# Third stage of a convolution block: the out-projection's second tile in banks of its own, ahead of the variance

## The chip, the cores and the metric

One core of one Trainium2 chip runs the whole program. The metric is the device time of one launch in microseconds; of the kernel before there are three timed runs, and their median is 3697.74 us (3695.79 to 3697.99). The profile shows one more execution. Engines are called TensorE (PE, with its weight loads as PEld), VectorE (DVE), ScalarE (ACT), GpSimd (POOL) and SyncE (SP, which only issues DMAs here).

## The reference

The input is 16 images of 192 channels, 64 x 64 pixels, float32. Cut to what matters:

```
h  = layernorm_channels(x)                       # first stage
p, g = split(conv1x1(h, in_proj))
p  = dwconv3(p)                                  # second stage
mixed = (scan in four directions(p) + dwconv3(p)) * sigmoid(g)
mixed = gelu(batchnorm(mixed))                   # third stage from here
x  = x + conv1x1(mixed, out_proj)                # 192 -> 192
h2 = layernorm_channels(x)
x  = x + conv1x1(gelu(conv1x1(h2, fc1)), fc2)    # 192 -> 768 -> 192
# second layer: per group of images a squeeze of the pooled x gives the
# taps of a masked 3x3 depthwise filter (4 taps are not masked)
pooled = mean(x);  t = relu(bn(pooled @ w1.T));  w = t @ w2.T + b2
out = depthwise(x, w) + bias
```

The first stage and the batch normalisation's statistics need all images before the third stage can begin; the pooled mean needs a whole image before its filter can.

## The kernel before

Three stages run one after the other. The first (to about 630 us) and the second (to about 1302 us) are not touched. The third works on pairs of images: the two images lie on partitions 0 to 63 and 64 to 127 (`HALF`), and the 192 channels are three tiles of 64 (t = 0, 1, 2). A chunk is 8 rows of 64 pixels, 512 columns (`CH`, its half `HCH`); there are 8 chunks a pair and 8 pairs, so 64 iterations of the main loop, from 1333 to about 3663 us, and then a tail with the last pair's filter.

Iteration n is a software pipeline. It holds, in the order in which it is written, which is the order on every engine's queue (the schedule is manual):

- `final(n - 1)`: VectorE adds the second MLP product of the previous chunk to the image (L992).
- `first(n, m)`, m = 0 to 5: TensorE multiplies the normalised h by 128 hidden channels (12 matmuls of 64 x 64 weights, each of which the trace shows as two, four running at a time in the quadrants), and ScalarE makes the GELU of it into `gl` (L972, L974). Each takes a pair of PSUM banks.
- between these: `mean` of chunk n + 1 (L928), `center` (L940), `squares` (L948 on ScalarE, L949 and L920 on VectorE).
- `unmix(n + 3)` and `load_mixed(n + 4)`: VectorE transposes and SP's DMAs for the mixed input of later chunks.
- `piece()`: one piece of the dynamic filter of an earlier pair, if there is one: a ScalarE step (L1029), three VectorE steps (L65), and output DMAs issued by GpSimd (L1033). Of the 64 iterations, 42 have a piece at this place, 42 one later (between the parts of `second`).
- the out-projection of chunk n + 2: `out_quarters` takes the 64 channels of the third input tile (64 x 64 weights, L890), `out_columns` the other 128 (128 x 64 weights, L897); each for three output tiles t, each output tile in two halves of 256 columns in two banks.
- `mean(n + 1, ..., "sq")`, the variance of chunk n + 1, in two banks called `ps_v` (L928).
- `load(n + 3)`: SP loads x.
- `squeeze`, when a pair has ended (eight times), L1006, L1008.
- `normalize(n + 1)`: ScalarE takes the square root of the variance (a table load and two steps, L958) and goes back to GELU's table (L960); VectorE takes the reciprocal (L961) and scales h (L962).
- `residual` of chunk n + 2: VectorE adds x and the bias to the out-projection, two steps a tile (L903), and makes the channel sums on the way (L909, L920).
- `bn_gelu(n + 3)`: ScalarE makes the GELU of the mixed input (L870, L871).
- `second(n, k)`, k = 0 to 2: the second MLP product, 128 x 64 weights, two hidden tiles m by three output tiles t in each (L843, the matmuls of `both`).

PSUM has eight banks here: tag `f1` two pairs, tag `f2` three single banks, tag `a` one. A tile taken under a tag gets the tag's next buffer in turn and waits for that buffer's last readers. In the kernel before, `f1` is taken eight times an iteration (six times by `first`, then twice for the out-projection: tiles 0 and 2 share one pair, tile 1 has the other, which the sixth `first` held last). `f2` is taken seven times: two for the mean, two for the variance, three for `second`. `a` serves the squeeze and the taps.

## Time and profile before

| | |
|---|---|
| median of three runs | 3697.74 us |
| profiled execution, its own time | 3699.46 us |
| its span, first to last instruction | 3697.7 us |
| granted TensorE clock | 0.995 |
| first and second stage | 0 to 1302 us |
| main loop of the third stage | 1333.2 to 3663.7 us |
| TensorE busy in the main loop | 2325.4 of 2330.5 us |
| VectorE busy in the main loop | 1529.1 us |
| ScalarE busy in the main loop | 951.7 us |
| one undisturbed iteration | 36.19 us |

In the lines of the profile, a group of instructions is given by source line, engine, operation and the program's names as output <- inputs; "x16" is how many were merged, and a bracket names how long the engine had been idle before and what released it. Starts count from the span's first instruction. Matmuls are pipelined and their ends are modelled, so that starts say more than lengths. "PEld" is the queue of weight loads, which runs ahead of the matmuls.

### The profile page before, as it was taken

Reading aid. Unit: us, or ns where it says so; the run is one execution under the profiler, and the core shown is the slowest. Engines: PE = TensorE matmul, PEld = TensorE weight load, DVE = VectorE, ACT = ScalarE, POOL = GpSimd, SP = SyncE. Lnnn points to the kernel's source line nnn. Section 1 sums busy time; section 2 is a strip of 40 time slices with the busy share of each in tenths; the row PEclk is TensorE's granted clock in tenths of the full one; section 3 lists DMA queues with packets and bytes.
Section 4 is the critical chain, followed back from the end, with each engine's and each line's share of the span. In section 5 each row is a group of like instructions: output and inputs, shape, how many; then the busy total and the mean of one; then the engine's idle time right before and its main releaser. Section 6 shows DMA issues by size and latency. Waiting matters only on the chain.

```text
span 3697.7 us, 71384 instructions
## 1 busy us (share of the span) xinstructions
PE 3670.5 (99%) x30354; PEld 1715.5 (46%) x30354; DVE 2705.5 (73%) x4138; ACT 1791.1 (48%) x2004; POOL 420.6 (11%) x685
## 2 busy tenths in 40 slices
PE   9999999999999999999999999999999999999998
PEld 6666666555566643333333334333333334333333
DVE  6878776999999965556766757766766676775764
ACT  3433333988888843434343434444443434343432
POOL 2434332111111020000000000000000000000000
PEclk9999999999999999999999999999999999999999
DMA  6898998999999941122212212221322231222212
GB/s 163 242 255 246 261 278 247 295 294 290 281 282 283 248 97 40 27 61 68 69 51 79 72 47 70 77 61 52 85 65 54 68 82 52 68 75 55 72 38 75
DMA packets 290335, 491.82 MB, mean 133 GB/s; under 512 B 26584, under 2 KB 184784, under 8 KB 290016
## 3 DMA queue, kind: packets, MB, share of 16 engines
q1 hardware_dynamic: 232540, 296.22, 30.1%
q0 software_dynamic: 56544, 189.99, 18.7%
q8 instruction: 240, 3.93, 0.5%
q10 hardware_dynamic: 932, 1.03, 0.1%
q14 instruction: 79, 0.65, 0.1%
HBM read 284.95 MB, written 197.92 MB: 131 GB/s over the span
## 4 chain that ended last, share of the span: by engine, by line
PE 98%; DMA 1%; DVE 1%; issue 0%; ACT 0%; SPq 0%; ACTq 0%; POOL 0%
PE ps_f L972 27%; PE ps_f L843 27%; PE ps_pj L514 14%; PE ps_l L673 11%; PE ps_d L629 7%; PE ps_o L897 5%; PE ps_o L890 3%; PE ps_xt L485 2%; PE ps_m L928 1%; PE ps_v L928 1%; DMA xa<-in_x_dram 1%; PE ps_k L843 0%; DVE o L65 0%; PE pb_h L141 0%; DVE ol L65 0%
## 5 line engine op out<-in xcount | busy, mean ns | idle before, releaser
L974 ACT ACTIVATE gl<-ps_f,bf 128x1024 f32<-128x1024 f32 x384 | 427.9, 1114 | 1308.4 <-PE ps_f L972 1302.8
L972 PE MATMUL ps_f<-h,wf 64*64 64x512 f32 x9216 | 1014.9, 590 | 2.0 <-DVE h L962 2.0
L843 PE MATMUL ps_f<-gl,place 128*64 128x512 f32 x4608 | 1003.6, 593 | 2.8 <-ACT rs L958 2.8
L972 PEld LDWEIGHTS ps_f<-h,wf 64*64 64x64 f32 x9216 | 346.3, 133 | 627.9 <-issue 566.0
L843 PEld LDWEIGHTS ps_f<-gl,place 128*64 128x64 f32 x4608 | 335.3, 137 | 627.1 <-issue 614.9
L514 PE MATMUL ps_pj<-wi,xa 64*128 64x384 f32 x3072 | 517.0, 489 | 1.4 <-DVE mid L519 1.0
L65 DVE SCALAR_TENSOR_TENSOR o<-ximg,taps,o 128x1024 f32<-128x1024 f32 (+1 forms) x267 | 338.2, 1267 | 111.0 <-ACT o L1029 101.1
L514 PEld LDWEIGHTS ps_pj<-wi,xa 64*128 64x128 f32 x3072 | 292.8, 188 | 197.3 <-issue 12.7
L1033 POOL DMA_DIRECT2D out_dram<-o x168 | 90.1, 541 | 2028.4 <-DVE o L65 2025.5
L940 DVE TENSOR_TENSOR h<-ximg,ps_m 128x768 f32<-128x768 f32 x128 | 116.4, 951 | 264.6 <-PE ps_m L928 263.4
L961 DVE RECIPROCAL rs<-rs 128x512 f32<-128x512 f32 x64 | 214.3, 3349 | 53.5 <-ACT rs L958 53.5
L992 DVE SCALAR_TENSOR_TENSOR ximg<-ps_f,pt,ximg 128x512 f32<-128x512 f32 x192 | 138.6, 750 | 133.9 <-PE ps_f L843 128.1
L664 DVE TENSOR_TENSOR_SCAN v<-tab,q 128x1024 f32<-128x1024 f32 x96 | 218.3, 2274 | 7.4 <-DMA pg_d<-mid 7.4
L666 DVE TENSOR_TENSOR_SCAN v<-tab,q 128x1024 f32<-128x1024 f32 x96 | 217.6, 2266 | 0.0
L652 ACT ACTIVATE tab<-mask,dec_b 128x1024 f32<-128x1024 f32 x192 | 209.9, 1147 | 0.0
L520 ACT ACTIVATE mid<-ps_pj,rsa 128x384 f32<-128x384 f32 x128 | 119.9, 938 | 185.5 <-PE ps_pj L514 179.2
L520 ACT ACTIVATE stg<-ps_pj,rsa 128x384 f32<-128x384 f32 x128 | 119.6, 936 | 182.3 <-PE ps_pj L514 175.5
L949 DVE TENSOR_TENSOR low<-low 128x512 f32<-128x512 f32 x63 | 43.6, 693 | 209.2 <-ACT low L948 209.2
L492 DVE BATCH_NORM_STATS2 st<-ps_xt 128x6 f32<-128x192 f32 x512 | 174.1, 340 | 16.1 <-PE ps_xt L485 15.3
L897 PE MATMUL ps_o<-low,wo 128*64 128x256 f32 x1536 | 181.8, 384 | 0.0
L243 DVE STREAM_TRANSPOSE low<-low 128x512 f32<-128x512 f32 x174 | 169.0, 1026 | 2.1 <-issue 0.3
L903 DVE SCALAR_TENSOR_TENSOR ximg<-ps_o,pt,low 128x256 f32<-128x256 f32 x384 | 161.7, 476 | 2.4 <-PE ps_o L890 2.3
(213 smaller groups left out, 4181.8 us busy)
## 6 DMA issues: line engine op xcount, KB each, us to landing
low<-in_x_dram SPq DMA_DIRECT2D x128, 384.0 KB
out_dram<-o POOLq DMA_DIRECT2D x168, 256.0 KB, 3.8
mid<-pg_d SPq DMA_DIRECT2D x8, 4096.0 KB
low<-mixed_d SPq DMA_DIRECT2D x116, 256.0 KB
low<-pg_d SPq DMA_DIRECT2D x7, 4096.0 KB
pg_o<-pg_d SPq DMA_DIRECT2D x7, 4096.0 KB
xa<-in_x_dram POOLq DMA_DIRECT2D x192, 128.0 KB, 5.4
xa<-in_x_dram SPq DMA_DIRECT2D x192, 128.0 KB
```

What stands on the lines that cost most here:

```text
L65: nc.vector.scalar_tensor_tensor(o, in0, scalar, in1, ALU.mult, ALU.add, **kw)
L514: nc.tensor.matmul(ps[i], pixels(n, t, g)[q], wi[q, t].rearrange("p g k c -> p (g k c)"), start=(t == 0), stop=(t == 2))
L520: nc.scalar.activation(stag[blk][1][:, :, j], ps[1], AF.Copy, scale=rs[:, g, 1:2])
L629: nc.tensor.matmul(dst(ps[o, ih]), mats[g % 2]["dm"][q, di + 1, :, ch], src(s["pg"][q, :, 0, ch]), start=(di == 0), stop=stop)
L664: nc.vector.tensor_tensor_scan(vf, tab, q, 0.0, ALU.mult, ALU.add)
L666: nc.vector.tensor_tensor_scan(vf[:, ::-1], tab[:, ::-1], q[:, ::-1], 0.0, ALU.mult, ALU.add)
L673: nc.tensor.matmul(dst(bst[k]["ps"][o, i]), lm_of(g)[q, m, :, c], src(q, ih), start=start, stop=stop)
L843: nc.tensor.matmul(ps[q], w(i), rhs(i), start=start, stop=stop)
L897: nc.tensor.matmul(ps[wh][q].rearrange("p (r w) -> p r w", w=32), wo[:, 64 * t:64 * t + 64], cols(rows(s["mx"][:, i]))[:, :, wh], start=fi ...
L961: nc.vector.reciprocal(rs, rs)
L972: nc.tensor.matmul(pf[o, i], wf1[q, t, m0:m0 + 64], s["h"][q, t], start=(t == 0), stop=(t == 2))
L974: nc.scalar.activation(gl, pf, AF.Gelu, bias=bf1[:, m:m + 1])
```

## The change

The sixth `first` moves behind `unmix`, `load_mixed` and the piece. The out-projection takes only one pair of `f1`, for tiles 0 and 2; tile 1 gets one bank of `f2` and the bank `a`. The quarters of tile 1 go ahead of the variance, those of tiles 0 and 2 behind it. The columns are taken in the order 1, 0, 2, and the residual of tile 1 goes ahead of `normalize`. The squeeze takes a pair of `f1` instead of bank `a`. `second` renames its three banks, so that the one that tile 1 of the out-projection held comes last, and its first third works tile by tile instead of hidden tile by hidden tile. `f1` is now taken seven times an iteration (eight with a squeeze), `f2` eight times. The channel sum is made after whichever of tiles 0 and 1 is added last. In iteration 0 the GELU of chunk 2's mixed input goes from behind the fifth `first` to behind the fourth.

```diff
@@ residual
-        if t == 1:
+        s["added"] = s.get("added", ()) + (t,)
+        if t < 2 and len(s["added"]) == 2:
             s["sum"] = hp2.tile([128, 3, HCH], F32, tag="sm", name="sm", bufs=1)
@@ second
+        gl = {m: s.pop(("gl", m)) for m in (2 * k, 2 * k + 1)}
         if k == 0:
-            s["po"] = [ps2.tile([128, CH], F32, tag="f2", name="ps_f2", bufs=3) for _ in range(3)]
-        for m in (2 * k, 2 * k + 1):
-            gl = s.pop(("gl", m))
-            for t in range(3):
-                both(s["po"][t], ..., m == 0, m == NFC - 1)
+            po = [ps2.tile([128, CH], F32, tag="f2", name="ps_f2", bufs=3) for _ in range(3)]
+            s["po"] = po[1:] + po[:1]
+            order = [(m, t) for t in range(3) for m in gl]
+        else:
+            order = [(m, t) for m in gl for t in range(3)]
+        for m, t in order:
+            both(s["po"][t], ..., m == 0, m == NFC - 1)
@@ squeeze
-        pt = ps2.tile([128, CH], F32, tag="a", name="ps_t")
+        pt = ps2.tile([128, 2, CH], F32, tag="f1", name="ps_t", bufs=2)[:, 0]
@@ main loop
-        for m in range(3, NFC):
+        for m in range(3, NFC - 1):
             at(first, n, m)
-            if n == 0 and m == 4:
+            if n == 0 and m == 3:
                 bn_gelu(2)
         at(unmix, n + 3)
         at(load_mixed, n + 4)
         piece()
+        at(first, n, NFC - 1)
         po = []
         if n + 2 < n_ch:
-            pair = [ps2.tile([128, 2, CH], F32, tag="f1", name="ps_o", bufs=2) for _ in range(2)]
-            po = [[pair[j][:, wh, c0:c0 + HCH] for wh in range(2)] for j, c0 in ((0, 0), (1, 0), (0, HCH))]
-            for t in (0, 2):
-                out_quarters(n + 2, t, po[t], True, t < 2)
+            own = [ps2.tile([128, CH], F32, tag="f2", name="ps_o1", bufs=3)[:, 0:HCH],
+                   ps2.tile([128, CH], F32, tag="a", name="ps_o1")[:, 0:HCH]]
+            pair = ps2.tile([128, 2, CH], F32, tag="f1", name="ps_o", bufs=2)
+            po = [[pair[:, wh, 0:HCH] for wh in range(2)], own, [pair[:, wh, HCH:CH] for wh in range(2)]]
+            out_quarters(n + 2, 1, po[1], True)
         if n + 1 < n_ch:
             st[n + 1]["pw"] = two_banks("ps_v")
             mean(n + 1, st[n + 1]["pw"], "sq")
         at(load, n + 3)
-        if n + 2 < n_ch:
-            out_quarters(n + 2, 1, po[1], True)
+        if po:
+            for t in (0, 2):
+                out_quarters(n + 2, t, po[t], True, t < 2)
         if ended is not None:
             squeeze(ended)
-        for t in range(len(po)):
-            out_columns(n + 2, t, po[t], False, t > 0)
+        if po:
+            for t in (1, 0, 2):
+                out_columns(n + 2, t, po[t], False, t > 0)
+            residual(n + 2, 1, po[1])
         at(normalize, n + 1)
-        for t in range(len(po)):
-            residual(n + 2, t, po[t])
+        if po:
+            for t in (0, 2):
+                residual(n + 2, t, po[t])
```

More of the change, by code (lines that the diff above doesn't have):

```diff
@@ L978, in second @@
         s = st[n]
+        gl = {m: s.pop(("gl", m)) for m in (2 * k, 2 * k + 1)}
         if k == 0:
-            s["po"] = [ps2.tile([128, CH], F32, tag="f2", name="ps_f2", bufs=3) for _ in range(3)]
-        for m in (2 * k, 2 * k + 1):
-            gl = s.pop(("gl", m))
-            for t in range(3):
-                both(s["po"][t], lambda i: wf2[:, m, 64 * t:64 * t + 64], lambda i: gl[:, i], m == 0, m == NFC - 1)
+            po = [ps2.tile([128, CH], F32, tag="f2", name="ps_f2", bufs=3) for _ in range(3)]
[4 more added lines that the diff above has]
+        for m, t in order:
+            both(s["po"][t], lambda i: wf2[:, m, 64 * t:64 * t + 64], lambda i: gl[m][:, i], m == 0, m == NFC - 1)
     def final(n):
```

## The prediction

> **What bounds the kernel now.** I read the page first: busy shares, then the chain that ended last.

> ```profile
> PE 3670.5 (99%) x30354; PEld 1715.5 (46%) x30354; DVE 2705.5 (73%) x4138; ACT 1791.1 (48%) x2004; POOL 420.6 (11%) x685
> ...
> PE 98%; DMA 1%; DVE 1%; issue 0%; ACT 0%; SPq 0%; ACTq 0%; POOL 0%
> ```

> TensorE sets the end, and the diff neither adds nor removes a matmul. So the change is worth the holes that it closes or opens in TensorE's stream, and the hole can be invisible in the busy share, because modelled matmul ends (376 ns each, while a group of four starts every 0.22 us) cover it. The weight loads show it better. Of the waits of PEld in the whole span, these belong to the third stage's loop:

> ```profile
> PEld ps_f L972 <- PE ps_f L843: 50.3, 62, 0.8
> PEld ps_o L890 <- ACT gl L974: 28.0, 61, 0.7
> PEld ps_f L843 <- ACT rs L958: 3.9, 2, 3.7
> ```

> The first stands at the turn from `second` to the next `first`, which the diff leaves alone. The second is the wait that the diff aims at: 61 times, 0.46 us each, of which a part would be idle anyway (loads run ahead of matmuls). How much is real, I read from the timeline of one iteration (n = 29), weight loads, then matmuls, then ScalarE; columns are start, length, engine, line.

> ```profile
> 2405.79 0.37 PEld L928 LDWEIGHTS ps_v<-low,mean 64*64 64x64 f32 x8
> 2406.61 0.21 PEld L890 LDWEIGHTS ps_o<-low,wo 64*64 64x64 f32 x8 [0.46 <-ACT gl L974]
> 2407.21 1.06 PEld L897 LDWEIGHTS ps_o<-low,wo 128*64 128x64 f32 x12 [0.38 <-issue]
> ```

> ```profile
> 2405.14 1.04 PE L890 MATMUL ps_o<-low,wo 64*64 64x256 f32 x16
> 2406.01 0.61 PE L928 MATMUL ps_v<-low,mean 64*64 64x256 f32 x8
> 2406.62 0.66 PE L890 MATMUL ps_o<-low,wo 64*64 64x256 f32 x8
> 2407.21 1.30 PE L897 MATMUL ps_o<-low,wo 128*64 128x256 f32 x10
> ```

> ```profile
> 2405.45 1.11 ACT L974 ACTIVATE gl<-ps_f,bf 128x1024 f32<-128x1024 f32 x1 [1.46 <-PE ps_f L972]
> 2406.46 1.23 ACT L1029 ACTIVATE o<-ximg,pt,taps 128x1024 f32<-128x1024 f32 x1
> 2407.71 1.28 ACT L958 ACT_TABLE_LOAD   x1
> 2409.01 0.84 ACT L958 ACTIVATE rs<-ps_v,eps 128x256 f32<-128x256 f32 x2
> ```

> Sixteen quarter matmuls (tiles 0 and 2) take 2406.01 - 2405.14 = 0.87, or 0.216 a group of four. The eight of the variance should take 0.43, but the next start is 0.61 later: the quarters of tile 1 wait for the sixth GELU, whose bank they take over and which ends at 2406.56. From variance to columns it is 1.20. The first iteration has the same instructions without that wait:

> ```profile
> 1350.72 0.61 PE L928 MATMUL ps_v<-low,mean 64*64 64x256 f32 x8
> 1351.16 0.61 PE L890 MATMUL ps_o<-low,wo 64*64 64x256 f32 x8
> 1351.70 2.81 PE L897 MATMUL ps_o<-low,wo 128*64 128x256 f32 x24
> ```

> There it is 0.98. The hole is thus 0.22 by these rounded starts (0.230 from the unrounded ones): 0.18 of waiting, 0.05 because the load behind the wait is no longer hidden. It is the same in every iteration from 1 to 61, with or without a piece of the dynamic filter; the period is 36.19.

> [...] the columns' first load (128 rows after 64) comes about 0.1 after the last quarter group's slot, in both samples; [...]. [...] The trace shows them in the order of the code, so the piece's ScalarE step, emitted ahead of the sixth GELU, runs ahead of it. [...] The load is 1.28 here; [...] (the square root follows 0.02 later), so I count 1.30.

> **The change, part by part** (t = 0 is the first quarter matmul, 2405.14 above).

> *Tile 1's quarters ahead, in banks of their own.* Removed: the wait. The order becomes quarters 1 (two groups), variance (two), quarters 0 and 2 (four), columns: 8 x 0.216 = 1.73, [...]. The pair of banks for 0 and 2 waits for the fifth GELU (2402.87 + 1.11 = 2403.98), done before t = 0. Tile 1's banks: one of the three of tag f2, last read by `final` at the iteration's start, some 13 us before; and the single bank of tag a, last read by tile 1's own residual or by the taps' addition a whole iteration before. No new wait. Gain 0.23 in each of 61 iterations: 14.0.

> *The variance, 0.43 earlier.* Its sums were ready 3.26 before it started in these iterations; now 2.83. Hidden.

> *Piece, unmix and mixed load ahead of the sixth `first`.* On TensorE nothing moves. On SP the loads keep their order, and SP never waits for `first`. POOL's output issues wait for the piece's VectorE steps and come up to 2 us earlier. On ScalarE the piece's step (1.23) goes to 2403.98-2405.21, a hole before the GELU at 2405.45: cover 0.24. Beyond it the GELU slips. VectorE's three piece steps start after the transposes, at 2405.68 instead of 2407.73.

> *Square root and `second`.* ScalarE: GELU till 1.42, table load till 2.72, square roots till 3.19 and 3.57. `second` now starts with a bank that the first square root reads, at 1.73 + 0.11 + 2.64 (columns, 2409.85 - 2407.21) = 4.48. Slack 1.29; nothing.

> *Residual of tile 1 ahead of the reciprocal.* VectorE: piece steps till 2409.60 (4.46), residual 0.95 till 5.4; its columns, first in order now, are done by about 3.1. The third tile of `second` takes over its bank at 4.48 + two tiles of 1.72 = 7.92: slack 2.5. The reciprocal starts at 5.4 rather than at 6.43 (2411.57), so the normalised h, needed 20 us after t = 0, is not late. The same additions are made; the residual moves past no queue other than VectorE's and issues no DMA.

> *Rotation of f2.* Eight takings an iteration instead of seven: the next means take the banks of tiles 2 and 0 of `second` instead of 0 and 1, so they wait for `final`'s last step, which ended at least 3.08 before the mean in every iteration. Hidden.

> *Squeeze in f1, eight times in all.* It takes the sixth GELU's bank at t = 1.73, free at 1.42 plus some 0.05. Hidden; seven of these iterations are among the 61 and gain alike.

> *Other order within `second`'s first third.* The same matmuls; consecutive ones already accumulate in one bank. I take 0; bounded by -1 to +3 over the run, an estimate from its 0.43 cadence, which shows no hole to lose or fill.

> *Iteration 0.* Its quarters start 0.65 late, at 1349.81, for the GELU of the mixed input (two steps, about 2.0), which the diff puts one GELU earlier, into a hole. Gain about 0.7. *Iteration 62* (no out-projection): `second` waits about 3.0 for the square root; the piece's step moves ahead of the GELU (1.2 gained), but `second` no longer has a free tile to begin with (0.86 lost). Gain 0.3.

> **Sum:** 14.0 + 0.7 + 0.3 = 15.0. On the profiled execution's span, 3697.7 - 15.0 = 3682.7 (its time was 3699.46, 1.8 around the span). The unprofiled median is 3697.74, so 3682.7 for it too: 0.41% faster. 0.2% (7.4 us) is about what a measurement of this kernel can tell from no change.

> **Rivals.** *(a) The square root takes the wait over.* If the piece's step still came between GELU and table load, the first square root would end at 3.47 + 0.87 + 0.47 = 4.81 against 4.48: a stall of 0.33, some 0.38 with the exposed load, in the 41 of the 61 iterations with a piece there: 15.6 lost, 3698. For it: it is the longest chain near the turn. Against: the 1.29 of slack, as ScalarE runs in order and its hole fits the step.

> *(b) Slower: the residual is late for its bank.* In-order VectorE reaches residual 1 after the piece's 3.92. Slack 2.5; beyond it each microsecond costs 41 us. It decides when the residual ends 3.1 later than reckoned: 0.6 x 41 = 24.6 eats the 15.0 and makes 3707. For it: two engines' orders meet there, and the bank is lent for the shortest time. Against: VectorE waited 2.04 for the piece's ScalarE step, and loses that wait.

> *(c) The change does not do what it says.* If the quarters met another unfinished reader, the gain would stay out: 3697. Against: the rotation counted above. *(d) Half:* the wait moves to the pair or the squeeze, or a refilled load pipeline costs the same again: 3690.

> **Chances.** Forecast 0.83 (3680 to 3687: 11 without the exposed load, 1 each for the rest, measuring noise of 1 to 2; up to 17 gained), (d) 0.06, (a) and (c) 0.05, (b) 0.06. Faster by over 0.2% is the forecast and half of (d), 0.86; within it the other half with (a) and (c), 0.08; slower 0.06. For 8 in 10, and because (d) starts where the forecast ends: 3679 to 3690.

> **What would show it.** Right: quarters in the order 1, variance, 0, 2 with no wait on a GELU; variance to columns 1.41 (0.43 + 0.87 + 0.11) and first quarter to columns 1.84 instead of 2.07; period 35.96; ScalarE's piece step ahead of the sixth GELU. Wrong: weight loads of `second` waiting for L958 or for a residual, of the means for L992, or ScalarE's sixth GELU starting late behind a piece that waits for its output buffer.

## The result and the profile after

The changed kernel takes 3676.51 us (median of five runs, 3674.51 to 3678.68) against 3696.90 us for the kernel before beside it (five runs): a ratio of 0.9945 with an interval of 0.9934 to 0.9956. It is faster by 0.55%, 20.4 us; the forecast was 15.0 us, with 3679 to 3690 for 8 in 10. A second set gave 3674.65 (five runs), with 3695.05 for the kernel before (13 runs): 20.4 again.

The page of the changed kernel, busy shares and the chain that ended last by engine:

```profile
PE 3649.8 (99%) x30354; PEld 1724.1 (47%) x30354; DVE 2713.3 (74%) x4138; ACT 1792.0 (49%) x2004; POOL 419.3 (11%) x685
...
PE 90%; DVE 1%; DMA 0%; issue 0%; ACT 0%; ACTq 0%; SPq 0%; POOL 0%; DVEq 0%
```

The number of matmuls is the same, and TensorE is still the bound. (The chain's 90%, where it was 98%, is no sign of a new bound: it is followed through less of the first stage, whose `ps_pj` has 7.5% of it instead of 13.5%.) Waits of the weight loads over the span, those of the third stage's loop:

```profile
PEld ps_f L973 <- DVE ximg L997: 51.1, 63, 0.8
PEld ps_t L1011 <- ACT gl L975: 2.7, 7, 0.4
PEld ps_f L843 <- ACT rs L959: 1.7, 1, 1.7
```

The row of 61 waits of `ps_o` for the GELU is gone. The first row is the turn from `second` to the next `first`; it was 50.3 in 62 waits and is now put down to `final` instead of to the matmuls, with the same 0.8 each. The 2.7 at the squeeze was there before too, but was put down to "issue", that is, to no wait that the profile shows. Iteration 29 again, matmuls and then ScalarE:

```profile
2393.03 0.61 PE L890 MATMUL ps_o<-low,wo 64*64 64x256 f32 x8
2393.46 0.61 PE L929 MATMUL ps_v<-low,mean 64*64 64x256 f32 x8
2393.89 1.04 PE L890 MATMUL ps_o<-low,wo 64*64 64x256 f32 x16
2394.86 2.81 PE L897 MATMUL ps_o<-low,wo 128*64 128x256 f32 x24
2397.50 4.89 PE L843 MATMUL ps_f<-gl,place 128*64 128x512 f32 x22
```

```profile
2391.77 1.23 ACT L1034 ACTIVATE o<-ximg,pt,taps 128x1024 f32<-128x1024 f32 x1
2393.33 1.12 ACT L975 ACTIVATE gl<-ps_f,bf 128x1024 f32<-128x1024 f32 x1 [0.33 <-PE ps_f L973]
2394.47 1.28 ACT L959 ACT_TABLE_LOAD   x1
2395.76 0.84 ACT L959 ACTIVATE rs<-ps_v,eps 128x256 f32<-128x256 f32 x2
```

First quarter to columns takes 1.83 instead of 2.07, the piece's step sits ahead of the sixth GELU, and the first square root is done at about 2396.2, some 1.3 before `second` starts.

Since the loop is so regular, the two traces can be subtracted iteration by iteration, from the start of one `first` to that of the next:

| part of the loop | before | after | difference |
|---|---|---|---|
| iteration 0 | 36.68 | 35.96 | -0.72 |
| an iteration from 1 to 61 (seven with a squeeze: 38.10, 37.87) | 36.19 | 35.96 | -0.23, in all -14.03 |
| iteration 13, on top of that | 0.28 | 0 | -0.28 |
| iteration 62 | 36.76 | 33.08 | -3.68 |
| iteration 63 | 35.85 | 35.93 | +0.08 |
| whole loop, to the first matmul of the tail's filter | 2330.51 | 2311.87 | -18.64 |

So 18.6 of the 20.4 lie in the loop, and iteration 62, which I had given 0.3, holds 3.68. The 0.28 of iteration 13 is a later sixth GELU in both traces of the kernel before. It comes with the piece's place behind that GELU: it is gone where the piece alone is moved, and back where the piece is put back (both below). What delays the GELU stays open. The stretch before the loop and the tail differ too, but they differ as much between two traces of one kernel: the loop began at 1333.2 and at 1326.7 in two traces of the kernel before, and the tail took 32.3 and 34.3 in two of the changed one. The 1.8 that are left are within the interval of the ratio; no run tells what they are.

### The profile page after: what moved, and what is told of

Read it like the earlier page. It is cut to its first block, busy times and chain, and to the rows that moved or that the text cites. A ratio compares the mean times of both kernels' runs of the same rounds, so it can differ in the third digit from the quotient of the medians.

```text
span 3672.7 us, 71322 instructions
## 1 busy us (share of the span) xinstructions
PE 3649.8 (99%) x30354; PEld 1724.1 (47%) x30354; DVE 2713.3 (74%) x4138; ACT 1792.0 (49%) x2004; POOL 419.3 (11%) x685
## 3 DMA queue, kind: packets, MB, share of 16 engines
q8 instruction: 239, 3.92, 0.5%
## 4 chain that ended last, share of the span: by engine, by line
PE 90%; DVE 1%; DMA 0%; issue 0%; ACT 0%; ACTq 0%; SPq 0%; POOL 0%; DVEq 0%
PE ps_f L973 27%; PE ps_f L843 27%; PE ps_l L673 11%; PE ps_pj L514 7%; PE ps_d L629 7%; PE ps_o L897 5%; PE ps_o L890 2%; PE ps_xt L485 1%; PE ps_m L929 1%; PE ps_v L929 1%; PE ps_k L843 0%; DMA xa<-in_x_dram 0%; DVE o L65 0%; PE pb_h L141 0%; DVE ol L65 0%
## 5 line engine op out<-in xcount | busy, mean ns | idle before, releaser
L843 PE MATMUL ps_f<-gl,place 128*64 128x512 f32 x4608 | 1001.9, 592 | 0.8 <-ACT rs L959 0.8
L843 PEld LDWEIGHTS ps_f<-gl,place 128*64 128x64 f32 x4608 | 334.9, 137 | 623.8 <-issue 613.9
L897 PE MATMUL ps_o<-low,wo 128*64 128x256 f32 x1536 | 182.0, 385 | 0.2 <-ACT low L870 0.2
```

The source lines that it names most:

```text
L843: nc.tensor.matmul(ps[q], w(i), rhs(i), start=start, stop=stop)
L897: nc.tensor.matmul(ps[wh][q].rearrange("p (r w) -> p r w", w=32), wo[:, 64 * t:64 * t + 64], cols(rows(s["mx"][:, i]))[:, :, wh], start=fi ...
```

## The experiments

A "stall" is here the distance from one start of TensorE's matmuls to the next, less the 0.43 that a group takes anyway; the expectations round the 2.93 of iteration 62 to 3.0.

*Theory after the result:* the steady part is as forecast; iteration 62 of the kernel before loses 2.9 to a wait for the square root, and then 1.7 more because TensorE's clock fell behind that wait. *Rivals:* the piece's new place, or the residual's, or the place of the quarters gains throughout the loop; the slow groups of iteration 62 are a refill of the pipeline; part of the gain is the luck of one profile.

**Part alone: the piece's place.** In the kernel before:

```diff
-        for m in range(3, NFC):
+        for m in range(3, NFC - 1):
             at(first, n, m)
-            if n == 0 and m == 4:
+            if n == 0 and m == 3:
...
         piece()
+        at(first, n, NFC - 1)
```

> The kernel before, with only the sixth `first` put behind the piece (and iteration 0's GELU of the mixed input one place earlier); banks and order of the out-projection as before. Theory (the hole is the wait for the sixth GELU's bank, and the clock fell after iteration 62's stall): the period stays 36.19, because the sixth GELU still ends 1.42 after the first quarter and tile 1 still waits; iteration 0 is 0.5 shorter; in iteration 62 the first square root ends 1.15 earlier, the stall shrinks from 3.0 to about 1.8, and if the clock then stays up another 1.7 goes: 2 to 4 us faster in all, about 3693.5 to 3695. Rival (the piece's place is what gains, by the earlier square root): a period near 35.96 and 3683 or less.

Measured: 3692.08 against 3696.02, ratio 0.9989 (0.9981 to 0.9998). The period stayed 36.19; iteration 0 took 36.13 (-0.55), iteration 62 took 33.94 (-2.82, that is 1.13 for the earlier square root and 1.69 because the clock, of which more below, stayed up). The weight loads of the quarters wait as before:

```profile
PEld ps_o L890 <- ACT gl L974: 28.3, 62, 0.5
```

So the place alone gains nothing in the steady loop, 3.4 at its two ends, and the 0.28 of iteration 13, which took 36.19 here. The time is 3.9 lower than that of the kernel before, inside the 2 to 4 that I had expected.

**Undone part: the piece behind the sixth `first`.** In the changed kernel, the sixth `first` goes back ahead of the piece (iteration 0's GELU of the mixed input stays where the change put it):

```diff
-        for m in range(3, NFC - 1):
+        for m in range(3, NFC):
...
         piece()
-        at(first, n, NFC - 1)
```

> The changed kernel, with the sixth `first` back ahead of the piece. Theory, from the trace's durations: in the 41 of 61 iterations with a piece there the first square root ends 4.81 after the first quarter, and `second` asks for its bank at 4.48, so TensorE stalls 0.33 to 0.38: period 36.3 there, 35.96 in the 20 without a piece; with some 1 to 3 more in iteration 62, 15 to 19 us slower than the changed kernel, 3691 to 3696. Rival (the order on ScalarE does not matter, slack covers it): 3676 to 3678 and a period of 35.96 throughout.

Measured: 3678.06, 1.55 above the changed kernel's first median, and a period of 35.96 except in iteration 13 (36.20). My expectation was wrong, and the rival right. The trace shows why (ScalarE, then a weight load of `second`):

```profile
2359.93 1.28 ACT L959 ACT_TABLE_LOAD   x1
2361.23 0.84 ACT L959 ACTIVATE rs<-ps_v,eps 128x256 f32<-128x256 f32 x2
```

```profile
2361.75 0.24 PEld L843 LDWEIGHTS ps_f<-gl,place 128*64 128x64 f32 x4 [0.20 <-ACT rs L959]
```

The first quarter of this iteration starts at 2357.36, so the first square root (0.47 of the 0.84) ends about 4.34 after it, not at 4.81: the 3.47 of my sum, counted from the variance, was already its end, and I had added its 0.47 once more. The weight load waits for it, but `second` still starts 2.64 after the columns, as ever. But hardly anything is left: in iteration 13, where the GELU came 0.28 late, `second` came 0.24 late. So the order on ScalarE is worth about 1.2 us of slack in the steady loop and no time, except in iteration 13; it is worth 1.13 in iteration 62, which took 34.20 here.

**Undone part: the quarters' place.** Changed kernel, with tile 1's quarters behind the variance and the other two, in banks of their own still:

```diff
-            out_quarters(n + 2, 1, po[1], True)
+            for t in (0, 2):
+                out_quarters(n + 2, t, po[t], True, t < 2)
...
         if po:
-            for t in (0, 2):
-                out_quarters(n + 2, t, po[t], True, t < 2)
+            out_quarters(n + 2, 1, po[1], True)
```

> The changed kernel, with tile 1's quarters at their old place, behind the variance and behind tiles 0 and 2, but still in the banks of their own. Theory (the bank makes the wait, not the place): no wait on a GELU, period 35.96, 3676.5 within 0.1%. Rival (the place ahead of the variance gains, because the variance or the square root comes sooner or later): a period that differs by 0.05 or more, above 3680.

Measured: 3677.41, period 35.96, no wait of `ps_o` for `gl`. The banks make the gain; that the quarters stand ahead of the variance adds nothing that can be seen. (Iteration 0 took 37.66, because a stretch of half clock, of which more below, fell into it.)

**Undone part: the residual's place.** Changed kernel, all three residuals behind the reciprocal and the scaling:

```diff
-            residual(n + 2, 1, po[1])
         at(normalize, n + 1)
         if po:
-            for t in (0, 2):
+            for t in (1, 0, 2):
                 residual(n + 2, t, po[t])
```

> The changed kernel, with the residual of tile 1 behind the reciprocal and the scaling, next to the other two. Theory of the lent bank: in iterations with a piece VectorE ends that residual at about 10.45 after the first quarter, and `second` asks for the bank at 7.92: a stall of 2.5 to 2.6 in 41 iterations (107), and of about 1.75 in the 20 without a piece (35): about 142 us slower, 3819. If stalls of that length also lower TensorE's clock, as I read iteration 62 of the kernel before, up to 1.7 more in each of the longer ones: 3819 to 3890. Rival (the residual's place is free, since VectorE has time): 3676 to 3680.

Measured: 3785.42, ratio 1.0245 (1.0229 to 1.0260), slower than the changed kernel by 109 (the loops of the two traces differ by 108.6) where I had expected about 142. Iterations with a piece took 37.97 (+2.01; only iteration 61 took less, 37.54), those without 37.30 (+1.34), those with a squeeze 38.94 (+1.07). VectorE and the weight loads of one iteration:

```profile
2370.39 3.35 DVE L962 RECIPROCAL rs<-rs 128x512 f32<-128x512 f32 x1
2373.77 1.76 DVE L963 TENSOR_TENSOR h<-h,rs 128x1536 f32<-128x1536 f32 x1
2375.45 1.65 DVE L903 SCALAR_TENSOR_TENSOR ximg<-ps_o,pt,low 128x256 f32<-128x256 f32 x4
```

```profile
2375.98 0.20 PEld L843 LDWEIGHTS ps_f<-gl,place 128*64 128x64 f32 x4 [2.68 <-DVE ximg L903]
```

The load goes on 0.53 after the residual's start, so it waits for the first of its two steps alone (0.48): the second step reads bank a, which `second` doesn't take. That is the 0.4 to 0.5 by which I had made the stalls too long; those with a squeeze, which I had not priced apart, are shorter still. The bank is lent at the price of this order: with the residual behind the reciprocal, the change would have been a loss of about 2.4%. None of the 40 stalls of 2.0 here lowered the clock; the granted clock is 1.0 from 1310.8 to 3747.9 in this trace.

**The clock: fill the gap.** In the kernel before, idle matmuls in iteration 62 alone, whose result nobody reads:

```diff
+        if n == n_ch - 2:
+            idle(3)
         at(normalize, n + 1)
```

> The kernel before, with three idle matmuls (128 x 128 weights, 512 columns, nobody reads their result) in iteration 62 alone, between the variance and `second`, inside the stall of 3.0. Theory (the stall lets TensorE's clock fall, and the half clock costs 1.7): the stall still ends with the first square root, but the groups behind it start every 0.43 at once, without the four starts of 0.86: iteration 62 is 1.5 to 1.8 shorter, 3695.3. It shows in the trace's granted clock around that place; in the median of the runs only if no other half-clock window comes and goes. Rival (the slow groups are a refill of the pipeline after the wait, whatever the clock): iteration 62 as long as before or up to 1 longer.

Measured: iteration 62 took 35.07 instead of 36.76: 1.70 shorter by the unrounded starts, with the weight load still waiting for the same square root. The median was 3693.21 against 3696.24, ratio 0.9993 (0.9985 to 1.0001), which alone would not tell. The weight loads of `second` in the second trace of the kernel before, and then in this one:

```profile
3604.86 0.20 PEld L843 LDWEIGHTS ps_f<-gl,place 128*64 128x64 f32 x4 [3.65 <-ACT rs L958]
3605.35 0.14 PEld L843 LDWEIGHTS ps_f<-gl,place 128*64 128x64 f32 x2 [0.28 <-ACT rs L958]
3605.95 0.24 PEld L843 LDWEIGHTS ps_f<-gl,place 128*64 128x64 f32 x2 [0.46 <-issue]
3606.81 0.24 PEld L843 LDWEIGHTS ps_f<-gl,place 128*64 128x64 f32 x2 [0.61 <-issue]
```

```profile
3608.46 0.20 PEld L843 LDWEIGHTS ps_f<-gl,place 128*64 128x64 f32 x4 [0.88 <-ACT rs L958]
3608.95 0.14 PEld L843 LDWEIGHTS ps_f<-gl,place 128*64 128x64 f32 x2 [0.29 <-ACT rs L958]
3609.38 0.14 PEld L843 LDWEIGHTS ps_f<-gl,place 128*64 128x64 f32 x2 [0.29 <-issue]
3609.80 0.14 PEld L843 LDWEIGHTS ps_f<-gl,place 128*64 128x64 f32 x2 [0.29 <-issue]
```

In the first, two loads come at the usual distance, and then the distance doubles to 0.86 and a load takes 0.24 instead of 0.14. The granted clock in the second trace of the kernel before, ahead of this stretch, in it and behind it (columns: window, length, busy time of PE, PEld, DVE, ACT and POOL, each with its number of instructions, then the clock, the DMA share and GB/s):

```profile
3602.18:3605.59 3.41, 0.72 (x4) 0.34 (x6) 2.49 (x2) 3.36 (x5) 0.00 (x0) 1.00 0.00 0
3605.60:3609.00 3.40, 3.40 (x10) 0.98 (x8) 3.36 (x3) 1.08 (x2) 1.07 (x2) 0.50 0.18 40
3609.00:3612.40 3.40, 3.40 (x18) 1.15 (x16) 3.01 (x2) 0.00 (x0) 0.00 (x0) 1.00 0.44 114
```

Half the clock for 3.41 costs 1.7. Against a refill of the pipeline: the first two loads behind the wait keep the usual distance, and behind the stall of 2.1 of the next experiment the pace is the usual one from the start, so that rival falls. Nor did the filled gap lie otherwise against the clock's steps of 3.41 (see the last section): it would have lain from 3605.69 to 3608.46, wholly inside one step (3605.13 to 3608.54, counted from the changes of the clock in that trace), as it lies, but for 0.09, in the kernel before.

**Part alone: tile by tile.** In the kernel before, only the order in `second`'s first third:

```diff
-        for m in (2 * k, 2 * k + 1):
-            gl = s.pop(("gl", m))
-            for t in range(3):
-                both(s["po"][t], ..., m == 0, m == NFC - 1)
+        gl = {m: s.pop(("gl", m)) for m in (2 * k, 2 * k + 1)}
+        order = [(m, t) for t in range(3) for m in gl] if k == 0 else [(m, t) for m in gl for t in range(3)]
+        for m, t in order:
+            both(s["po"][t], ..., m == 0, m == NFC - 1)
```

> The kernel before, with only the order in the first third of `second` changed: tile by tile. Theory: no hole anywhere but in iteration 62, so a period of 36.19; in iteration 62 two blocks instead of one run before the wait for the first square root, so that it is 0.86 shorter, and 2.5 if the stall of 2.1 that is left no longer lowers the clock: 3696.0 or 3694.4. Rival (consecutive accumulation into one bank costs): a longer period, from 36.2 up.

Measured: 3693.21 against 3696.24, ratio 0.9991 (0.9983 to 1.0000). The period stayed 36.19 and iteration 62 took 34.21 (-2.55): 0.86 for the second block ahead of the wait, and 1.69 because the clock stayed up over the 2.07 that were left of it.

**Both kernels again, and the ends.** The last of the three runs adds to the changed kernel a free bank in iteration 62 and two idle matmuls in the tail:

```diff
             s["po"] = po[1:] + po[:1]
+            if n == n_ch - 2:
+                s["po"][1] = ps2.tile([128, CH], F32, tag="a", name="ps_f2")
...
             squeeze(ended)
+            if ended == n_pairs - 1:
+                idle(1)
...
             excite(ended)
+            if ended == n_pairs - 1:
+                fill = ps2.tile([128, CH], F32, tag="f2", name="ps_i", bufs=3)
+                nc.tensor.matmul(fill, ident, wf1[:, 0, 0:CH], start=True, stop=True)
```

> The kernel before once more, as it is. Theory: a period of 36.19; in iteration 62 the stall of 3.0 comes again, and the half clock behind it comes again if the stall is what lowers it (36.76), so that its loop is 18.4 longer than the changed kernel's; with the clock up, iteration 62 would be 35.1 and the loop 16.7 longer. Median 3696.

> The changed kernel once more, as it is. Theory: the loop from the first iteration to the tail takes 2311.9 again (61 periods of 35.96, seven of them 37.87, iteration 62 about 33.1), since nothing in it depends on luck; the tail takes 32.3 if TensorE's clock stays up at its start and 33.9 to 34.7 if it falls there, as in every other trace but this kernel's first. Median 3676.5 to 3678. Rival (part of the gain over the forecast is the luck of one profile): a longer loop, or a median at 3680 or above.

> The changed kernel with two additions outside the steady loop: in iteration 62 the second tile of `second` takes bank a, which is free there, and in the tail one idle matmul behind the last squeeze and one behind the last taps fill TensorE's two gaps. Theory: iteration 62 loses its stall of 1.05 (32.0 instead of 33.1); the clock no longer falls at the tail's start, so that the tail from its first filter matmul takes about 32.3 in every trace; the taps come up to 0.3 later for the idle matmul ahead of them. In all 1 to 2.5 faster than the changed kernel beside it, which the runs can hardly tell. Rival (the clock at the tail's start has nothing to do with those gaps): a half-clock window there again and a tail of 33.5 or more.

The kernel before took 3695.05, and its loop is the same 2330.51, with 36.76 in iteration 62. The changed kernel took 3674.65. The loop of its trace is 2314.24, but the period and iteration 62 (33.08) are the same, and the 2.4 more are half clock in iteration 0 (1.70) and at the end of iteration 63 (0.67). So the expectation of 2311.9 "since nothing in it depends on luck" was too strong: half clock fell into both ends of the loop here, and into neither in this kernel's first trace. Its tail took 34.29, with a half clock at its start. In the version with additions at both ends, iteration 62 took 32.08 and there was no half clock at the tail's start, but the two idle matmuls cost 0.76 (in iteration 63) and 0.55 (in the tail, 32.89 long), and the median of 3676.02 cannot be told from 3674.65. It is no better version by these runs. Nor does its one trace show that the fillers kept the clock up: the first trace of the changed kernel, without them, has no half clock there either.

## Why the prediction was wrong in size

- **The hole.** Forecast 0.23 in each of 61 iterations, 14.0; measured 0.230, 14.03. (It was not quite the same in all of them, as I had said: iteration 13 had 0.28 more to gain.) Reading it from the first iteration, which has the same instructions without the wait, gave the exposed weight load too (0.05), which the wait alone (0.18) would have missed.
- **The covers.** The variance, the pair of banks, the rotation of `f2`, the squeeze and the output loads stayed hidden as forecast. The 0.11 that I had counted ahead of the columns is there after the change too, 0.10 by the rounded starts: 0.97 from the first of the last four quarter groups to the columns (2393.89 to 2394.86), where four groups take 0.87. Square root to `second`: 1.29 forecast, about 1.3 measured.
- **Iteration 0.** Forecast 0.7, measured 0.72.
- **The step that failed is iteration 62, "Gain 0.3"; it measured 3.68.** It has two errors. I counted 1.2 for the earlier square root, which measured 1.13, and took off 0.86, "`second` no longer has a free tile to begin with". It has. Before (the kernel's first trace), and then after (its second), TensorE's start of `second` in iteration 62:

```profile
3607.57 1.08 PE L843 MATMUL ps_f<-gl,place 128*64 128x512 f32 x4
3611.42 16.51 PE L843 MATMUL ps_f<-gl,place 128*64 128x512 f32 x68 [2.77 <-ACT rs L958]
```

```profile
3591.09 1.94 PE L843 MATMUL ps_f<-gl,place 128*64 128x512 f32 x8
3593.81 13.95 PE L843 MATMUL ps_f<-gl,place 128*64 128x512 f32 x64 [0.78 <-ACT rs L959]
```

Eight matmuls, two blocks, run before the wait, where four, one block, ran before. So the 0.86 is a gain. I had reckoned with three banks that are handed out strictly in turn, by which the first tile would have had to wait. The trace names no banks, so why a free one comes first there stays open. The piece's place alone gave the 1.13 and the order tile by tile alone the 0.86; together they take the stall from 2.93 to 0.94. The other 1.7 I left out altogether: behind the stall of 2.93 the clock falls to half for 3.41, and in no other trace does it fall behind what is left of that stall (2.07 or less). 1.13 + 0.86 + 1.69 = 3.68.

That can be read in the trace of before, two lines behind the wait that I quoted; I took its length and did not look at the pace behind it. In both traces of the kernel before, TensorE was busy for 0.72 or 0.73 of the 3.41 ahead of the fall, and the half clock lasted 3.41.
- **The range.** It gave 1 us to each of the other terms, and no term for the clock. With 3.4 more in iteration 62 the sum is 18.4, or 3679.3 from the median that I started from; the lower end should have left room below that. The measured 3676.51 lies another 2.8 lower: 0.8 because the kernel before took 3696.90 beside it and not 3697.74, 0.3 in iteration 13, and 1.7 that no run explains.
- **Rival (a)** was priced wrongly by one square root (0.47): it would not have decided at 4.34 against 4.48, though only some 0.1 was left. **Rival (b)** was the right danger in the right place; its slack was 0.5 larger than I had made it, and undoing the order cost 109. **(c)** and **(d)** did not happen.

## What to carry to other kernels

When the bounding engine is 99% busy, subtract starts: a regular iteration against one that happens to lack the wait shows the hole, down to the load that the wait exposes. Price the irregular iterations with the same care, one by one, and look at the pace behind each long wait as well as at its length: here a stall of 2.9 cost 1.7 more, because the clock fell behind it. And a bank that is lent is free in time only if the queue that empties it comes to it early enough: here the wrong order on VectorE turned a gain of 20 into a loss of 89.

## What the runs showed of the hardware that I had not expected

Between them lies a gap of 2.01 ahead of the loop, where TensorE waits for the first h in all eleven traces. In nine of them the clock stays up; in two, the second of the changed kernel and that with the quarters at their old place, it falls, and iteration 0 is 1.70 longer. The step with the gap and the one behind it, in the second trace of the changed kernel, then in the version with additions at both ends; and the same around iteration 62 with tile by tile:

```profile
1327.83:1331.24 3.41, 1.40 (x13) 0.51 (x16) 3.34 (x5) 0.00 (x0) 0.51 (x1) 1.00 1.06 168
1331.24:1334.65 3.41, 3.41 (x20) 1.07 (x16) 2.80 (x8) 0.27 (x1) 1.81 (x3) 0.50 1.10 174
```

```profile
1327.73:1331.14 3.41, 1.41 (x16) 0.59 (x20) 3.34 (x6) 0.00 (x0) 1.05 (x2) 1.00 1.18 176
1331.14:1334.55 3.41, 3.41 (x40) 1.23 (x36) 2.58 (x8) 1.11 (x1) 2.44 (x5) 1.00 1.07 185
```

```profile
3604.46:3607.87 3.41, 1.50 (x8) 0.34 (x6) 2.24 (x2) 3.36 (x5) 0.00 (x0) 1.00 0.00 0
3607.87:3611.28 3.41, 3.41 (x18) 1.15 (x16) 3.37 (x3) 1.35 (x2) 1.07 (x2) 1.00 0.13 29
```

In the two that fell, the gap began 0.22 and 0.93 behind the start of a step and so lay wholly in that step. In the nine others it began at the start of a step (the second pair of lines) or up to 1.15 ahead of one, and most were divided by it. Which gaps lower the clock, beyond the one that was filled, is not shown: no run moved one gap against the steps and left the rest alone, and at the start of the tail the clock falls in most traces behind steps in which TensorE was busy for more than half of the time (2.22 of the 3.41 in the first trace of the kernel before). Such stretches of half clock at the head and the tail come in one trace of a kernel and not in the next. They are a part of why the spans of one kernel differ by several microseconds while its steady loop repeats to the hundredth: of the 5.9 between the spans of the changed kernel's two traces (3672.7 and 3678.6), the 2.4 in the loop are half clock.
